# A two-layer graph network on one core: layer 0 started on half of the adjacency, the second group's neighbour lists made beside the first group's attention

## The chip, the core and the metric

The kernel runs on one core of a Trainium2 chip. A core has five engines that run beside each other, each working through its own queue of instructions in order: TensorE (PE in the profile; its weight loads are PEld), VectorE (DVE), ScalarE (ACT), GpSimd (POOL) and SyncE (SP, which here only issues DMAs). Data moves between HBM and on-chip memory by 16 DMA engines; a DMA can be issued from SP, ACT or POOL. The metric is device time in microseconds (us), and smaller is better.

## The reference

There are 3327 nodes with 512 features each and a symmetric 0/1 adjacency with self loops, about nine neighbours a node. Two layers follow each other, each with a residual and a layer norm.

```python
# layer 0: graph attention, 4 heads of 128
feats = einsum('nf,hfo->hno', x, W)
logits = leaky_relu(e_self[:, :, None] + e_neigh[:, None, :], 0.2), masked by adj
out0 = relu(concat_h(softmax(logits) @ feats) + b)
x = layernorm(x + out0)
# layer 1: a gated pair
attn_a = sigmoid(concat(adj @ x, x) @ Wa.T + ba);  attn_b likewise with Wb, bb
x_a = normalised(exp(-leaky_relu(s_left[:, None] + s_right[None, :], 0.01)) * adj) @ (x @ W_sa)
x_b = adj @ (x @ W_gcnb) + b_gcnb
x = layernorm(x + sigmoid(attn_a * x_a + attn_b * x_b))
```

All arithmetic that reaches the output is in float32.

## The kernel before, in words

The nodes, padded to 3328, are 26 tiles of 128. The kernel does not multiply with the adjacency: it turns it into lists of neighbours and gathers rows.

**First stage.** SP loads x (chunks of 512 nodes, three buffers, `load_x`) and the adjacency (`load_adj`, L197, chunks of 512 columns, each in 13 pairs of 128-row blocks, twelve buffers, so a pair is loaded when an earlier one has been used). TensorE does two kinds of work: `features(t)` (L307) projects tile t on the four heads and on the score columns, ScalarE copies the result out of PSUM, and POOL writes it as a row of 520 numbers to `table0` in HBM (L321); `make_codes(i)` (L333) sums the adjacency of chunk i into codes that hold 8 rows' bits and a block number, and `turn_codes` (L355) transposes them so that a node is a partition. VectorE then finds each node's neighbours: `top_codes` (L365, three rounds of the eight greatest, over 224 codes), `decode` (L371) and `pick` (L389, three rounds again, over 96 candidates), up to 24 neighbours a node. All 26 tiles go through this before attention.

**Groups and lists.** Nodes fall into two groups, the first 12 tiles (group 0) and the other 14 (group 1). In a group the nodes are sorted by number of neighbours: `rank_a` and `rank_b` (L416, L426) work out ranks on VectorE with two matmuls, `sort` (L455) scatters each list to its rank in HBM (one POOL scatter a tile, L137), and a DMA loads the sorted lists into `srt`. Sorted tile j needs only `CAPS[j]` neighbours a node: 22 for the first tile of each group, 4 or 5 for the last. For group 0 the x rows of the sorted nodes are gathered as well (`own_x`, L463, 12 POOL gathers); for group 1 SP copies x and the table rows side by side into `own1` (L512, L513), so that one gather brings both.

**Layer 0.** `gather(table0, j)` (L525) issues one indirect DMA on POOL for each neighbour slot (L546; L540 for the slot that comes from `own1`): 128 rows of 520 numbers. A buffer holds up to 6 slots, and there are 7 buffers. In iteration i of the loop at L689 the kernel emits, in this order: the gather of the tile three ahead; for finished groups of up to four tiles the `publish` (L656: ScalarE normalises, POOL scatters the row to `table1`); `columns2` of tile i-2; `attend` of tile i (L619: each row is multiplied with its weight on VectorE, every third one on ScalarE at L629, and TensorE adds it up in PSUM with an identity matmul, L634); for tile i-1 the residual (L704), the statistics and `columns1` (transposes); `columns3`; and the weighing of tile i+1 (`weigh_a`, `weigh_b`, L599: leaky ReLU and softmax of the scores). The order of the tiles is 11, 10, 0 to 9, 12 to 25. Each engine keeps this order, so an instruction that waits holds all behind it on its engine.

Group 1's list scatters are issued at L668, after the gathers of the first three tiles. Behind them the buffers of the first stage are given back, and VectorE clears `over` (L676) in their place.

**Layer 1.** The same gathers from `table1`, in another order of tiles; weights and gates on VectorE, sums on VectorE and TensorE, two projections by W_sa and W_gcnb (L831), and a scatter of the rows to the output. `covered` (L468) checks on the chip that no list was cut; if one was, a dense version of everything runs instead.

Of the kernel before, what the change touches and what calls it, by code (L numbers as in the profile page):

```python
# [34 lines left out]
CH = 512  # L35

# [40 lines left out]
def sparse_pass(  # L77
# [3 lines left out]
    x: bass.AP,  # L81
# [32 lines left out]

    nc = tc.nc
    N, F = out.shape
    NP = x.shape[0]
# [12 lines left out]
    table0 = dram.tile([NP, ROW], F32, name="table0")  # L130
    table1 = dram.tile([NP, ROW], F32, name="table1")
# [26 lines left out]
    selves = const.tile([P, NT], F32, name="selves")  # L158

# [4 lines left out]
    def own(j):  # L164
        g, i = place(j)
        return srt[g][:, i, 0:1]
# [30 lines left out]
    def load_adj(i):  # L197
        cw = min(CH, NP - chunks[i])
        for q, (a, b) in enumerate(pairs_of(NT)):
            at = p0.tile([P, 2, CH], F32, tag="at", name=f"at{i}_{a}", bufs=AT)  # L200
            nc.sync.dma_start(at[:, :, :cw], adjB[i, q] if cw == CH else adjL[q])

            ones_of = at.bitcast(BF16).rearrange("p t (n w) -> p t n w", w=2)[:, :, :cw, 1]
            loaded[i, a], loaded[i, b] = ones_of[:, 0], ones_of[:, 1]

    load_x(0)
    wsa0 = pj.tile([P, KT, F], F32, name="wsa0")
    nc.scalar.dma_start(wsa0, W_sa.rearrange("(k p) o -> p k o", p=P))
    asa_rows = []
    for s in range(2):  # L210
        a_row = pj.tile([P, F], F32, name=f"asa_row{s}")
        nc.scalar.dma_start(a_row, row_bcast(a_sa, F, s * F))
        asa_rows.append(a_row)
    load_x(1)
    for i in range(len(chunks)):
        load_adj(i)
        load_x(i + 2)
# [40 lines left out]
    nc.gpsimd.iota(st[:, :, 0], pattern=[[P, NT]], base=0, channel_multiplier=1)  # L258
    for g, n in enumerate(NG):
# [16 lines left out]
    nc.gpsimd.dma_start(table1[N:NP, :], zrow)  # L276
# [3 lines left out]

    nc.gpsimd.memset(v1, 0.0)
# [14 lines left out]
    for s in range(2):  # L296
        for k in range(KT):
            prod = pj.tile([P, F], F32, tag="prod1", name=f"sprod{s}_{k}", bufs=2)
            nc.gpsimd.tensor_mul(prod, wsa0[:, k], asa_rows[s])
            nc.vector.tensor_reduce(v1[:, k, 3 - 3 * s : 4 - 3 * s], prod, AX.X, ALU.add)  # L300

    nc.gpsimd.tensor_add(v1[:, :, 4:6], v1[:, :, 4:6], v1[:, :, 1:3])
    nc.gpsimd.tensor_add(v1[:, :, 6], v1[:, :, 0], v1[:, :, 3])

    deg = [p0.tile([P, n], F32, name=f"deg{i}") for i, n in enumerate(NG)]

    def features(t):  # L307

        i = t * P // CH
        xc = xcs[i]  # L310
        o = t * P - chunks[i]
        pf = psf.tile([P, 2, 512], F32, tag="pf", name=f"pf{t}")
        for k, hh in ((k, hh) for hh in range(2) for k in range(KT)):
            nc.tensor.matmul(  # L314
                pf[:, hh, :HC], xc[:, k, o : o + P], w0[:, k, hh, :], start=(k == 0), stop=(k == KT - 1)
            )
# [4 lines left out]
        nc.gpsimd.dma_start(table0[t * P : (t + 1) * P, :], row)  # L321
        if t == NT - 1:
            nc.gpsimd.dma_start(table0[N:NP, F : F + H], nrow[:, F : F + H])
# [4 lines left out]
    def span(i):  # L328

        t0 = chunks[i] // P  # L330
        return (t0, min(CH, NP - chunks[i]) // P, *place(t0))

    def make_codes(i):  # L333
# [3 lines left out]
        for half, ms in enumerate(halves):  # L337
            pc = psl.tile([P, CH], F32, tag=f"pc{half}", name=f"pc{half}_{i}")
            for m in ms:
# [5 lines left out]
                if s == 0 and own0 // 4 == m // 4:  # L345
                    for j in range(nt):
                        nc.tensor.matmul(
                            pc[32 * c : 32 * c + 32, j * P : (j + 1) * P], pow2[:, j, :], less1, start=False, stop=False
                        )
            w = widths[half]  # L350
            nc.scalar.activation(
                v[:w, half, : nt * P], pc[:w, : nt * P], AF.Identity, bias=blk[:w, half : half + 1]
            )
# [11 lines left out]
    def top_codes(i):  # L365

        ent = ents[i] = p0.tile([P, 4, S], F32, tag="ent", name=f"ent{i}", bufs=2)
        for j in range(span(i)[1]):
# [20 lines left out]
    def pick(i):  # L389
# [22 lines left out]
        nc.vector.tensor_scalar(st[:, t0 : t0 + nt, 1 : S + 1], some[:, :nt], float(N), None, ALU.add)  # L412
# [42 lines left out]
    def sort(g, ranki, queue):  # L455
# [4 lines left out]
        if g == 0:  # L460
            tasks.extend(lambda j=j: own_x(j) for j in range(NG[0]))

    def own_x(j):  # L463
        nc.gpsimd.indirect_dma_start(
            out=row1(j)[:, 0:F], out_offset=None, in_=x, in_offset=bass.IndirectOffsetOnAxis(ap=own(j), axis=0)
        )

    def covered():  # L468

        for g, n in enumerate(NG):  # L470
            nc.vector.tensor_scalar(valid[:, T0[g] : T0[g] + n, :], srt[g][:, :, 1 : S + 1], N, None, ALU.is_lt)
# [3 lines left out]
        nc.vector.tensor_mul(over, over, valid)  # L475
# [4 lines left out]
        pb = psx.tile([P, NCOL], F32, tag="pcol", name="pbad", bufs=2)  # L480
# [4 lines left out]
    ts = iter(range(NT))  # L485

    def more(n):
        for _ in range(n):
            t = next(ts, None)
            if t is not None:  # L490
                features(t)
                later(3)

    NC0 = NG[0] * P // CH
    assert NG[0] * P % CH == 0
    more(3)
    rankis = [None, None]
    for i in range(len(chunks)):
        make_codes(i)
        more(1)  # L500
        if i == NC0:
            rankis[0] = rank_b(0)
            sort(0, rankis[0], nc.gpsimd)
# [4 lines left out]
        if i == NC0 - 1:  # L508
            rank_a(0)
# [827 lines left out]
```

## Time and profile before

| what | value |
|---|---|
| median of 3 runs (lowest, highest) | 1033.98 us (1031.57 to 1038.35) |
| profiled execution, own time | 1029.15 us |
| its span, first to last instruction | 1027.4 us |
| busy share of the span | PE 79%, DVE 71%, POOL 64%, ACT 27% |
| mean granted TensorE clock | 0.899 |
| adjacency loads (L201) | 78 of 512 KB and 13 of 256 KB, issued from SP |
| gathers L546 | 496 on POOL, 1025 ns each, 508.2 us |
| first gather L546; first attention matmul L634 | 177.0 us; 246.7 us |
| last attention matmuls of layer 0 | from 589.0 us |

A line of the groups names the source line, the engine, the operation, what it writes and reads with shapes, how often, then the busy time and mean duration of one, and the idle time of that engine just before with what ended it. In a timeline each line is a start time, a length, the engine, the line and operation, and in brackets the idle time before it and its releaser; "issue" means that nothing the profile shows was waited for. A wait line gives who waited for whom, the total, how often, and the longest. The span starts at 0.

### The profile page before, as it was taken

The page shows a single profiled execution, that of the slowest core. Times are in us where ns is not written, and L with a number is a line of the kernel's source. Part 1 is how long each engine was busy: PE and PEld are TensorE (multiplying, and loading weights), DVE is VectorE, ACT ScalarE, POOL GpSimd, SP SyncE. Part 2 cuts the span into 40 slices and gives each one's busy share as a digit, 9 for nine tenths or more (in the row PEclk, how much of TensorE's full clock was granted, in tenths as well). Part 3 has the DMA queues.
Part 4 walks back from the last instruction along what each step waited for, and adds up shares of the span by engine and source line. Part 5 has one row for each costly group of instructions (what it writes and reads, how often), then busy time and mean ns, then how long its engine had stood idle before and what let it go on. Part 6 is the DMA issues. An engine that isn't in the chain of part 4 may idle for free.

```text
span 1027.4 us, 10026 instructions
## 1 busy us (share of the span) xinstructions
PE 810.6 (79%) x2564; PEld 420.8 (41%) x2564; DVE 732.5 (71%) x2128; ACT 273.9 (27%) x751; POOL 658.2 (64%) x673
## 2 busy tenths in 40 slices
PE   4698974203999983999699939996996989999994
PEld 3477751101444441444344414443442444444342
DVE  4387898704866760957466848886986989989894
ACT  1112210002344340353334413331131132232223
POOL 6411246773777777777777657777677677777602
PEclk9799995555999997899989969998998999999998
DMA  8999999993777678777777547778578566667501
GB/s 318 395 361 398 365 369 386 368 256 97 206 210 208 205 213 193 241 228 227 216 233 226 182 127 196 195 194 202 159 196 205 157 189 187 191 195 192 178 0 64
DMA packets 74193, 229.31 MB, mean 223 GB/s; under 512 B 13872, under 2 KB 18144, under 8 KB 73232
## 3 DMA queue, kind: packets, MB, share of 16 engines
q0 software_dynamic: 50240, 164.52, 55.8%
q1 hardware_dynamic: 22784, 61.97, 15.9%
q10 hardware_dynamic: 1104, 2.10, 0.6%
q8 instruction: 23, 0.38, 0.1%
q14 instruction: 42, 0.34, 0.1%
HBM read 207.46 MB, written 28.54 MB: 230 GB/s over the span
## 4 chain that ended last, share of the span: by engine, by line
PE 32%; POOL 12%; DMA 10%; issue 10%; DVE 9%; ACT 3%; DVEq 0%; POOLq 0%; ACTq 0%
PE acc L634 17%; POOL g L546 10%; DMA g<-table,srt 10%; PE acc L812 5%; PE po L831 4%; DVE sw L795 3%; PE pcol L650 2%; PE acc L623 2%; POOL out L137 1%; DVE g L797 1%; ACT xt L647 1%; PE pt L822 1%; PE x1t L643 1%; ACT za L872 1%; POOL g L540 1%
## 5 line engine op out<-in xcount | busy, mean ns | idle before, releaser
L546 POOL DMA_INDIRECT g<-table,srt x496 | 508.2, 1025 | 174.7 <-issue 128.3
L634 PE MATMUL acc<-g,ident 128*128 128x512 f32 x536 | 242.4, 608 | 41.1 <-DVE g L631 41.1
L795 DVE SCALAR_TENSOR_TENSOR sw<-g,e,sw 128x512 f32<-128x512 f32 x242 | 181.4, 749 | 16.4 <-ACT sw L784 11.8
L634 PEld LDWEIGHTS acc<-g,ident 128*128 128x128 f32 x536 | 105.0, 196 | 176.6 <-issue 107.4
L812 PE MATMUL acc<-g,ident 128*128 128x512 f32 x294 | 140.6, 610 | 20.3 <-DVE g L797 20.1
L631 DVE TENSOR_TENSOR g<-g,w 128x512 f32<-128x512 f32 x188 | 118.4, 698 | 0.7
L314 PE MATMUL pf<-w,xc 128*128 128x260 f32 x416 | 99.1, 399 | 13.5 <-DVE w L272 13.5
L629 ACT ACTIVATE g<-g,w 128x128 f32<-128x128 f32 x320 | 96.3, 389 | 1.9 <-DVE w L617 1.9
L812 PEld LDWEIGHTS acc<-g,ident 128*128 128x128 f32 x294 | 55.8, 194 | 99.0 <-issue 54.2
L831 PE MATMUL po<-wg,sT 128*128 128x512 f32 x208 | 94.7, 598 | 0.0
L831 PE MATMUL po<-wsa,sT 128*128 128x512 f32 x208 | 93.9, 594 | 0.2 <-ACT sT L824 0.2
L314 PEld LDWEIGHTS pf<-w,xc 128*128 128x128 f32 x416 | 81.4, 198 | 28.7 <-DVE w L272 14.3
L797 DVE TENSOR_TENSOR g<-g 128x512 f32<-128x512 f32 x95 | 65.7, 692 | 3.3
L650 PE MATMUL pcol<-v,xt 128*128 128x8 f32 x208 | 29.6, 269 | 46.6 <-ACT xt L647 46.6
L321 POOL DMA_DIRECT2D table<-row x26 | 14.4, 555 | 79.2 <-ACT st L320 79.2
L605 DVE TENSOR_TENSOR w<-g,srt 128x20 f32<-128x20 f32 (+3 forms) x57 | 9.9, 181 | 76.6 <-DMA g<-table,srt 71.3
L858 ACT ACTIVATE za<-za 128x512 f32<-128x512 f32 x26 | 16.4, 633 | 167.9 <-DVE za L856 167.9
L831 PEld LDWEIGHTS po<-wg,sT 128*128 128x128 f32 x208 | 40.1, 193 | 50.9 <-issue 50.6
L831 PEld LDWEIGHTS po<-wsa,sT 128*128 128x128 f32 x208 | 39.7, 191 | 50.4 <-issue 48.2
L137 POOL DMA_INDIRECT out<-za,srt x26 | 28.5, 1095 | 49.7 <-ACT za L872 43.0
L341 PE MATMUL pc<-at,pow 128*32 128x512 bf16 (+1 forms) x182 | 26.2, 421 | 31.9 <-DMA at<-in_adjB 25.3
L610 ACT ACTIVATE w<-w 128x40 f32<-128x40 f32 (+10 forms) x26 | 6.2, 237 | 166.5 <-DVE w L609 166.3
(186 smaller groups left out, 916.7 us busy)
## 6 DMA issues: line engine op xcount, KB each, us to landing
at<-in_adjB SPq DMA_DIRECT2D x78, 512.0 KB, 11.9
g<-table,srt POOLq DMA_INDIRECT x496, 3.8
table<-row POOLq DMA_DIRECT2D x26, 260.0 KB, 6.5
xc<-in_xB SPq DMA_DIRECT2D x6, 1024.0 KB, 9.6
own<-in_xo SPq DMA_DIRECT2D x1, 3640.0 KB, 32.4
own<-table SPq DMA_DIRECT2D x1, 3640.0 KB, 55.4
at<-in_adjL SPq DMA_DIRECT2D x13, 256.0 KB, 8.9
w<-in_W0B SPq DMA_DIRECT2D x1, 1040.0 KB, 6.9
```

Of the source, the lines that this page charges most:

```text
L137: put = nc.gpsimd.indirect_dma_start(out=dst, out_offset=bass.IndirectOffsetOnAxis(ap=rows, axis=0), in_=src, in_offset=None, bounds_check ...
L314: nc.tensor.matmul(pf[:, hh, :HC], xc[:, k, o : o + P], w0[:, k, hh, :], start=(k == 0), stop=(k == KT - 1))
L341: nc.tensor.matmul(pc[32 * c : 32 * c + 32, : nt * P], pow2[:, s, :], loaded[i, m], start=(s == 0), stop=(m + 1 not in ms or s == 3),)
L546: nc.gpsimd.indirect_dma_start(out=buf[:, q - q0, :], out_offset=None, in_=table[:, :], in_offset=bass.IndirectOffsetOnAxis(ap=srt[g][:, i ...
L629: nc.scalar.activation(gv[:, h, :], gv[:, h, :], AF.Copy, scale=w[:, s, h : h + 1])
L631: nc.vector.tensor_tensor(gv, gv, w[:, s, :].rearrange("p (h o) -> p h o", o=1).to_broadcast([P, H, FO]), ALU.mult)
L634: nc.tensor.matmul(acc, ident, buf[:, o + s - s0, 0:F], start=False, stop=(s == CAPS[j]))
L650: nc.tensor.matmul(pcol, xt1[:, k, :], v1[:, k, :], start=(k == 0), stop=(k == KT - 1))
L795: nc.vector.scalar_tensor_tensor(sw, g[:, i, 0:F], e[:, s : s + 1], sw, ALU.mult, ALU.add)
L797: nc.vector.tensor_add(g[:, i, 0:F], g[:, i - 1, 0:F], g[:, i, 0:F])
L812: nc.tensor.matmul(plain[j], ident, row, start=(not sums_of_two and i == 0), stop=(sums_of_two and i == len(rows) - 1),)
L831: nc.tensor.matmul(proj[j], sT[:, k, :], wt[:, k, :], start=(half + k == 0), stop=(half + k == KT))
```

## The change

1. The adjacency is cut into chunks of 4, 4, 2, 2, 4, 4, 4, 2 tiles of columns (`CT`); the first four are group 0. Only these are turned into codes and lists in the first stage. A generator yields after each pair of blocks, and a table `PACE` says how many pairs TensorE takes ahead of each feature tile. SP's loads are put in a fixed order that mixes x and adjacency; `wsa0` and `asa_row` move from ACT's queue to SP's, behind all x chunks. The layer-1 columns (`sprod`) are made by 4 products on POOL instead of 8 and at tile 20 instead of the start; their sums follow the ranking of group 0.
2. Chunks 4 to 7 (group 1) are turned into codes and lists inside the layer-0 loop, in iterations 1 to 6, and ranked and sorted in iteration 7 (`beside`). They stand behind `columns3` and ahead of the weighing of the next tile.
3. For group 0 the table holds x and features of a node in adjacent rows (`by_node`), x copied there by one DMA, and group 0's gather takes both with one indirect DMA, as group 1's does from `own1`. `own_x` is gone. Group 1's rows are written twice by POOL, to the table and to `own1`, and the copy at L513 is gone. The rows of x that layer 1 doesn't fill are set to ones by two DMAs.
4. In group 0 every second row is multiplied on ScalarE, instead of every third.
5. `over` is cleared by POOL at the start. The PSUM pool of the layer-0 columns has one buffer until group 1 is sorted, then two.

```diff
+CT = (4, 4, 2, 2, 4, 4, 4, 2)
+PACE = (0, 0, 0, 1, 3, 6, 8, 10, 13, 14, 17, 20, 23, 26, 29, 32, 36, 41, 45, 49, 52)
...
-    table0 = dram.tile([NP, ROW], F32, name="table0")
+    table0 = dram.tile([NP + R0, ROW], F32, name="table0")
+    by_node = [table[: 2 * R0].rearrange("(n t) w -> n t w", t=2) for table in (table0, table1)]
...
     load_x(0)
+    load_x(1)
+    load_adj(0)
+    load_x(2)
+    load_adj(1)
+    load_x(3)
+    load_x(4)
+    load_adj(2)
+    load_adj(3)
...
+    load_x(5)
+    load_x(6)
+    nc.sync.dma_start(wsa0, W_sa.rearrange("(k p) o -> p k o", p=P))
     for s in range(2):
+        nc.sync.dma_start(asa_rows[s], row_bcast(a_sa, F, s * F))
-    load_x(1)
-    for i in range(len(chunks)):
-        load_adj(i)
-        load_x(i + 2)
...
+    def columns_a():
+        for s, k in ((s, k) for s in range(2) for k in range(0, KT, 2)):
+            prod = sprods[s, k] = pj.tile([P, 2, F], F32, tag="prod", name=f"sprod{s}_{k}", bufs=4)
+            nc.gpsimd.tensor_mul(
+                prod, wsa0[:, k : k + 2], asa_rows[s].rearrange("p (k o) -> p k o", k=1).to_broadcast([P, 2, F])
+            )
...
-        nc.gpsimd.dma_start(table0[t * P : (t + 1) * P, :], row)
+        if t < NG[0]:
+            nc.gpsimd.dma_start(by_node[0][t * P : (t + 1) * P, 1, :], row)
+        else:
+            nc.gpsimd.dma_start(table0[R0 + t * P : R0 + (t + 1) * P, :], row)
+            nc.gpsimd.dma_start(own1[t * P - R0 : (t + 1) * P - R0, 1, :], row)
...
-        if g == 0:
-            tasks.extend(lambda j=j: own_x(j) for j in range(NG[0]))
...
+    nc.sync.dma_start(by_node[0][:, 0, :], xo[:R0])
+    for i in range(G0, len(CT)):
+        load_adj(i)
...
+    nc.sync.dma_start(own1[:, 0, :], xo[R0:])
...
+    for t in range(NT):
+        while pairs < PACE[min(t, len(PACE) - 1)]:
+            next(steps)
+            pairs += 1
...
+        if t < 2:
+            project0(t, F // 2, HC)
+        else:
+            project0(t, 0, HC)
+        features(t)
+        later(3)
+        if turning is not None:
+            lists_of(turning)
+            if turning == G0 - 1:
+                columns_a()
+                rank_a(0)
+            turning = None
+        if t == NT - 2:
+            rankis[0] = rank_b(0)
+            sort(0, rankis[0], nc.gpsimd)
+            columns_b()
...
-        ahead = 0 if table is table1 else 1 + g
+        ahead = 0 if table is table1 else 2
+        pairs, word = (by_node[0], 0) if g == 0 else (own1, S + 1)
...
-                if s % 3 == 2:
+                if s % (2 + (j >= NG[0])) == 1:
...
+    def codes_and(i, j1):
+        make_codes(i)
+        turn_codes(i)
+        top_codes(i, 0, j1)
+
+    def ends_of(i, j0):
+        top_codes(i, j0)
+        decode(i)
+        pick(i)
+
+    def sort1():
+        rank_a(1)
+        rankis[1] = rank_b(1)
+        sort(1, rankis[1], nc.sync)
+        later(len(tasks))
...
+    beside = {
+        1: lambda: codes_and(4, 2), 2: lambda: ends_of(4, 2), 3: lambda: codes_and(5, 2), 4: lambda: ends_of(5, 2),
+        5: lambda: codes_and(6, 2), 6: lambda: (ends_of(6, 2), codes_and(7, 2), ends_of(7, 2)), 7: sort1,
+    }
...
-            xj = y if j < NG[0] else got[j][0][2][:, 0, 0:F]
-            nc.vector.scalar_tensor_tensor(y, accs[j], 0.0, xj, ALU.max, ALU.add)
+            nc.vector.scalar_tensor_tensor(y, accs[j], 0.0, got[j][0][2][:, 0, 0:F], ALU.max, ALU.add)
...
         if 2 <= i < NT + 2:
             columns3(order0[i - 2])
+        if i in beside:
+            beside[i]()
         if i + 1 < NT:
             weigh_a(order0[i + 1])
             weigh_b(order0[i + 1])
```

## The prediction

> **What bounds the kernel now.** I read the page first, then the busy time by stretches, then GpSimd's (POOL's) timeline, then VectorE's (DVE's) timeline inside one adjacency chunk. The stretches are: 177 us (first neighbour gather) to the first attention matmul, layer 0 on group 0, layer 0 on group 1.
>
> ```profile
> 177.00:244.00 67.00, 7.52 (x18) 3.83 (x18) 23.47 (x122) 0.40 (x1) 48.83 (x50) 0.50 0.83 261
> 246.70:416.50 169.80, 141.81 (x407) 69.62 (x408) 103.08 (x278) 62.22 (x194) 123.09 (x126) 0.92 0.74 207
> 416.50:600.00 183.50, 163.27 (x493) 81.55 (x491) 126.95 (x394) 70.53 (x204) 131.07 (x132) 0.96 0.69 210
> ```
>
> Columns: stretch, length, busy PE, PE weight load, DVE, ACT, POOL, PE clock, DMA share, GB/s. From 177 to 244 TensorE and VectorE do almost nothing while POOL issues. VectorE is 61% busy in group 0, so nothing there runs it full.
>
> ```profile
> 176.98 0.96 POOL L546 DMA_INDIRECT g<-table,srt  x1 [0.30 <-issue]
> 178.25 0.95 POOL L546 DMA_INDIRECT g<-table,srt  x1 [0.30 <-issue]
> ...
> 255.33 0.99 POOL L546 DMA_INDIRECT g<-table,srt  x1 [14.58 <-PE acc L634]
> ...
> 375.18 0.95 POOL L540 DMA_INDIRECT g<-own,srt  x1 [0.30 <-DMA g<-table,srt]
> ```
>
> One gather costs POOL 1.26 us (start to start). Between 177 and 375 POOL stood still once, 14.58 us, for a buffer. So tile 12, the first of group 1, begins to be gathered at 375.2, and POOL goes on at the same step to about 580. Up to there POOL sets the pace; it had 36 gathers ahead when attention began, because VectorE was held:
>
> ```profile
> DVE over L676 <- issue: 39.6, 1, 39.6
> DVE ent L69 <- PE pv L361: 20.0, 4, 11.0
> ```
>
> The first line is the clearing of `over`, which waits for POOL's 14 list scatters; the second is the list search waiting for TensorE's transposes, also when a chunk had TensorE to itself. What the lists cost VectorE:
>
> ```profile
> 69.62 0.40 DVE L69 MAX8 ent<-pv 128x8 f32<-128x224 f32 x1 [2.64 <-PE pv L361]
> ...
> 78.31 0.29 DVE L376 CAST bn<-ent 128x96 int32<-128x96 f32 x1
> ...
> 81.99 0.25 DVE L392 TENSOR_REDUCE ovf<-code 128x4 f32<-128x96 f32 x1
> ...
> 89.87 0.21 DVE L412 TENSOR_SCALAR st<-some 128x96 int32<-128x96 f32 x1
> ```
>
> A chunk of four tiles takes 20.5 us without a gap: search 8.7 (2.17 a tile), decode 3.7, pick 8.1. In the first stage this hides under the load of the adjacency.
>
> **What the Trainium skill says.** Perfetto Trace Analysis, Sequencer Loop: instructions wait in their engine's queue for their semaphores. The trace agrees: one waiting clear at L676 held VectorE 39.6 us. DMA: Bandwidth & Descriptors, Anatomy of one DMA: a DMA's semaphore wait is done on the issuing sequencer; here POOL's 14.58 us. The same page, Issuing engines are not separate DMA queues: all engines' transfers interleave on the same 16. The trace agrees: beside loads and copies (177 to 222) a gather landed after 8.1 us (median), alone (270 to 370) after 3.7, at the same issue step. TensorE: Matmul & The Clock Gate, What's actually happening: an idle window of about 3.4 us halves the clock. Here, after 41 us idle, 6 rows took 8.34 us, the next 7 rows 6.17.
>
> **The change part by part.**
>
> *First stage.* 14 of 26 adjacency columns leave it. TensorE keeps 26 feature tiles (four took 14.22, so 3.56 each: 92), codes for 12 tiles (about 8), their transposes (3); starting at 9 instead of 12.9 (the first two tiles no longer wait for the score columns), 112. DMA keeps 1.0 MB of W0, 6.7 of x, 20 of adjacency, about 8.5 of row writes and vectors: 36 MB at 375 GB/s (mean of 25 to 175 us) is 97, plus 5, so the last x chunks land near 102 and their six tiles end at 122 at worst. I take 118. Then, in POOL's queue: copies out 0.9, row writes 1.1, the wait of the padding row for the last row 6.0 + 0.6, 12 scatters at 1.27 (15.3), 2.7 for their landing, list load 1.1 + 6.3: 34. The columns for layer 1 (4 products of 1024 at 2.45) now sit in that queue behind a late weight load: 0 to 10, I take 5. First gather 157 (148 to 163) instead of 177: 20 us earlier. The 12 gathers of x rows (12 x 1.26) and the SP copy of table rows go; they stood before 177, in that figure. The clears on POOL at the start (27, of 0.2) are covered by its 79.2 us of waiting for row copies.
>
> *Self rows.* One gather now brings x and features, so the count per tile stays (CAPS+1), but a group-0 tile takes CAPS+2 slots: tiles 10 and 11 together 4 buffers instead of 3. Its first buffer is also held until L704 reads x, after the next tile's multiplications.
>
> *Attention split.* In group 0 half of the rows instead of a third go to ScalarE: 4.78 us for 4 rows, 1.2 each, hidden under TensorE's 0.86 a row. VectorE: 0.64 a row.
>
> *Lists of group 1 beside attention.* In VectorE's order they stand between L704 of tile i-1 and the weighing of tile i+1, so all attention behind them waits. Durations are from VectorE's and TensorE's timelines between 284 and 305 us: L704 0.69, statistics 0.87, column copy 0.17; weighing 9 short instructions, 2.0 to 2.2 with ScalarE's exponential; norm 2.6; TensorE 0.86 a row (46 half matmuls in 19.74); ranking from the rows of L420 to L445, 0.5 and 4.2 plus gaps. Tile 0's gather (the 36th) is issued at 157 + 36 x 1.26 = 202, lands 7 later, and is weighed at 211. From there VectorE works, per iteration (rows x 0.64 + 1.8 for L704, statistics and column copy + 2.2 weighing + lists + norm or publish):
> i=2: 7.7+4.0+16.1 = 27.8. i=3: 4.5+4.0+4.3 = 12.8. i=4: 3.8+4.0+16.1+2.6 = 26.5. i=5: 3.8+4.0+4.3 = 12.1. i=6: 3.2+4.0+1.8+16.1+12.6 = 37.7. i=7, to the end of ranking: 3.2+1.8+0.5+4.5 = 10.0. Sum 127. In four of them it also waits for TensorE, because codes and transposes stand in TensorE's queue behind the whole attention of tile i. At i=3: 13 rows (11.2) + first row and its transposes 2.5 + codes, copy and turn 4 = 18, less VectorE's 6.5 until then: 11. At i=5 likewise 10, at i=6 0, at i=7 7 (10 rows 8.6 + 3 - 5). 28. Two adjacency chunks come through what the gathers leave (390 - 207 = 183 GB/s; 13 pairs are 37 us) and add some 2.5 each: 5. TensorE is idle for 8 to 25 us before tiles 1, 3, 5 and starts at half clock, 2 each: 6. Ranking ends at 211 + 127 + 28 + 5 + 6 = 377.
>
> *POOL behind it.* 14 scatters wait for the ranking: 17.8, then tile 9's 7 gathers 8.8, so tile 12 starts at 404 instead of 375: 29 later. SP loads the new lists while those 7 gathers run. Tile 12 then meets fewer free buffers, since held ones come free only with the next tile: 5 for tile 13. After that the order is that of before. The end check does a pass less on VectorE (0.6), nothing else in layer 1 changes.
>
> Sum: -20 at the first gather, +49 by tile 12, +5 buffers: +34. Profiled execution 1029.15 (span 1027.4) becomes 1063. The median of the runs, 1033.98, is 4.8 above that execution: 1068.
>
> **Rivals.**
>
> *The same, with DMA as a second bound* (0.19). For: 0.74 of DMA is taken by gathers alone, and some 24 MB of adjacency and fills come on top. Gathers land at 9 instead of 7 and only 140 GB/s are left: +12 to +25, so 1080 to 1093. Against: from 177 to 222 the loads beside gathers left the issue step at 1.26.
>
> *The lists overlap* (0.17): VectorE never waits for TensorE. Then ranking is at 211 + 127 = 338, tile 12 at 365, -10 and 5 for buffers: 1029. With the first gather at 148 instead of 157 it is 1020, faster. It decides from the point where at most a fifth of the 39 us of waits is left. Against: L69 already waited for the transposes.
>
> *POOL stays the bound* (0.06), the other side: nothing holds POOL from the first gather on. 148 + 125 x 1.26 + 8 publishes x 1.3 + 14 scatters 17.8 = 334 for tile 12 instead of 375: 993. It needs the ranking by 316, that is 105 us of VectorE after tile 0, where the list has 127.
>
> *The change doesn't shorten the first stage* (0.03): TensorE's and POOL's order give nothing, first gather at 177: 1088.
>
> **How the numbers follow.** The likeliest (0.55) is 1068, own range 1050 to 1085. About 1% is what a measurement here tells from no change: 1023.6 to 1044.3. Faster: POOL bound 0.06 and a quarter of the overlap, 0.10. Same: the rest of the overlap and a little of the likeliest, 0.14. Slower 0.76. Range 1036 to 1096, leaving out POOL bound, most of the overlap and small tails.
>
> **What would show it.** First gather at 148 to 163, first attention matmul near 175; VectorE over 85% busy from tile 0 to the ranking, with waits of 6 to 12 us of L69 for `pv`; TensorE idle before tiles 3, 5, 6 and 7; POOL waiting over 20 us ahead of the list scatters; L540's group-1 gathers from about 404; layer 1 as long as before. It is wrong if POOL's step stays unbroken, or if the first stage ends more than 15 us from 157.

## The result, and the profile after

The changed kernel takes 1082.6 us (median of 4 runs, 1077.72 to 1083.34), the kernel before beside it 1034.24: ratio 1.045 (95% interval 1.041 to 1.050), 48 us slower. Its profiled execution took 1081.86 us with a span of 1080.1, against 1029.15 and 1027.4 before. The kernels below ran on several chips. On those of a2, e4, e5, e6, f2, f3 and g1 the kernel before took 1033.5 or 1033.6 us; they are called the faster chips. e1, e2, e3 and f1 ran on a slower chip (kernel before: 1137.56 us) and f5 on another slower one (1134.12 us). Ratios are to the kernel before on the same chip, and the kernel before has no trace on the slower chips. The ratios leave out runs that took over 1.5% longer than the fastest of their kernel, which came up on the slower chips only, while the medians hold all runs.

First POOL's timeline in the changed kernel, at the four places that the prediction priced.

```profile
162.25 1.01 POOL L612 DMA_INDIRECT g<-table,srt  x1 [3.60 <-DMA srt<-lists]
...
389.63 1.00 POOL L146 DMA_INDIRECT lists<-st,ranki  x1 [0.37 <-DVE w L677]
...
407.38 0.97 POOL L146 DMA_INDIRECT lists<-st,ranki  x1 [0.30 <-issue]
...
417.71 0.95 POOL L612 DMA_INDIRECT g<-own,srt  x1 [0.30 <-issue]
...
465.70 0.95 POOL L618 DMA_INDIRECT g<-table,srt  x1 [7.27 <-DVE x1a L789]
```

The first gather starts at 162.25 (predicted 157; before 176.98), group 1's list scatters at 389.63 (predicted 377), tile 12 at 417.71 (predicted 404; before 375.18). Later, at 465.70, POOL stands 7.27 us for a first buffer that the residual L789 still holds. The last attention matmuls of layer 0, in the changed kernel and in the kernel before:

```profile
641.55 4.46 PE L706 MATMUL acc<-g,ident 128*128 128x512 f32 x10
```

```profile
589.00 4.45 PE L634 MATMUL acc<-g,ident 128*128 128x512 f32 x10
```

They end at 646.0 instead of 593.5. From there to the end both kernels take the same: 434.1 and 433.9 us. So the whole loss, 52.7 us by the spans, arises before layer 1, and since the first gather is 15 us earlier, layer 0 from its first gather on takes 67 us longer.

Then the busy time by stretches of the changed kernel (columns as in the prediction): first gather, tile 0 weighed, half of the list work, ranking done, tile 12, end of layer 0.

```profile
162.00:223.00 61.00, 20.14 (x72) 9.51 (x72) 15.08 (x50) 9.80 (x30) 42.65 (x45) 0.61 0.89 246
223.00:305.00 82.00, 58.86 (x176) 28.82 (x175) 60.34 (x226) 30.03 (x99) 45.24 (x48) 0.83 0.94 344
305.00:389.00 84.00, 50.70 (x178) 26.11 (x178) 53.78 (x200) 24.99 (x74) 28.74 (x30) 0.74 0.61 195
389.00:418.00 29.00, 25.14 (x75) 13.31 (x76) 22.37 (x73) 16.51 (x50) 22.24 (x23) 0.88 0.38 110
418.00:646.00 228.00, 183.88 (x529) 91.21 (x528) 127.43 (x391) 86.85 (x264) 162.01 (x163) 0.90 0.72 215
```

From 223 to 389 POOL, which stood still once on this way in the kernel before, works 74 us of 166 and VectorE 114. Neither is full: the queues wait for each other. The waits from 162 to 440 say which:

```profile
DVE ent L72 <- PE pv L408: 45.3, 4, 16.3
...
POOL g L612 <- DVE x1a L789: 33.4, 4, 13.5
...
POOL g L618 <- DVE x1a L789: 16.3, 2, 8.3
PE pc L380 <- DMA at<-in_adjB: 12.0, 3, 5.1
...
DVE tots L489 <- PE tot L485: 9.4, 1, 9.4
```

Each of the four chunks has one long wait of the list search (L72) for TensorE's transposes (L408), except the last with 0.43. While VectorE stands there, the residual and the weighing behind it in its queue stand too, so buffers stay full and POOL waits for L789.

### The profile page after: what moved, and what is told of

It is laid out like the page before. It is cut to its first block, busy times and chain, and to the rows that moved or that the text cites. A ratio compares the mean times of both kernels' runs of the same rounds, so it can differ in the third digit from the quotient of the medians.

```text
span 1080.1 us, 10313 instructions
## 1 busy us (share of the span) xinstructions
PE 828.4 (77%) x2622; PEld 434.0 (40%) x2622; DVE 720.5 (67%) x2106; ACT 306.3 (28%) x865; POOL 654.2 (61%) x698
## 4 chain that ended last, share of the span: by engine, by line
PE 33%; POOL 20%; issue 17%; DMA 14%; DVE 12%; ACT 3%; POOLq 0%; DVEq 0%; ACTq 0%; SPq 0%
POOL g L618 15%; DMA g<-table,srt 12%; PE acc L706 11%; PE pf L343 6%; PE acc L899 5%; PE po L918 5%; POOL lists L146 2%; PE pcol L722 2%; PE acc L695 2%; DVE sw L882 2%; DVE ent L72 1%; DVE topv L75 1%; ACT xt L719 1%; POOL out L146 1%; DMA xc<-in_xB 1%
## 5 line engine op out<-in xcount | busy, mean ns | idle before, releaser
L618 POOL DMA_INDIRECT g<-table,srt x484 | 497.1, 1027 | 200.9 <-issue 139.8
L706 PE MATMUL acc<-g,ident 128*128 128x512 f32 x536 | 251.5, 627 | 37.6 <-DMA g<-table,srt 37.6
L706 PEld LDWEIGHTS acc<-g,ident 128*128 128x128 f32 x536 | 109.5, 205 | 182.3 <-issue 150.4
L899 PE MATMUL acc<-g,ident 128*128 128x512 f32 x294 | 141.9, 615 | 20.3 <-DVE g L884 20.2
L701 ACT ACTIVATE g<-g,w 128x128 f32<-128x128 f32 x432 | 129.0, 389 | 3.8 <-DVE w L689 2.6
L722 PE MATMUL pcol<-v,xt 128*128 128x8 f32 x208 | 35.4, 298 | 115.2 <-ACT xt L719 115.2
L343 PE MATMUL pf<-w,xc 128*128 128x260 f32 (+2 forms) x448 | 103.5, 386 | 10.8 <-DMA xc<-in_xB 10.8
L677 DVE TENSOR_TENSOR w<-g,srt 128x20 f32<-128x20 f32 (+3 forms) x59 | 10.5, 181 | 134.9 <-DMA g<-table,srt 133.9
L703 DVE TENSOR_TENSOR g<-g,w 128x512 f32<-128x512 f32 x160 | 99.7, 691 | 0.7
L899 PEld LDWEIGHTS acc<-g,ident 128*128 128x128 f32 x294 | 56.3, 196 | 99.8 <-issue 55.2
L343 PEld LDWEIGHTS pf<-w,xc 128*128 128x128 f32 x448 | 83.6, 196 | 28.1 <-issue 15.8
L722 PEld LDWEIGHTS pcol<-v,xt 128*128 128x128 f32 x208 | 33.0, 242 | 122.0 <-ACT xt L719 122.0
L72 DVE MAX8 ent<-pv 128x8 f32<-128x224 f32 x26 | 10.1, 387 | 82.7 <-PE pv L408 82.7
```

The source lines that it names most:

```text
L343: nc.tensor.matmul(pfs[t][:, hh, n0:n1], xcs[i][:, k, o : o + P], w0[:, k, hh, n0:n1], start=(k == 0), stop=(k == KT - 1),)
L618: nc.gpsimd.indirect_dma_start(out=buf[:, q - q0, :], out_offset=None, in_=table[:, :], in_offset=bass.IndirectOffsetOnAxis(ap=srt[g][:, i ...
L701: nc.scalar.activation(gv[:, h, :], gv[:, h, :], AF.Copy, scale=w[:, s, h : h + 1])
L703: nc.vector.tensor_tensor(gv, gv, w[:, s, :].rearrange("p (h o) -> p h o", o=1).to_broadcast([P, H, FO]), ALU.mult)
L706: nc.tensor.matmul(acc, ident, buf[:, o + s - s0, 0:F], start=False, stop=(s == CAPS[j]))
L722: nc.tensor.matmul(pcol, xt1[:, k, :], v1[:, k, :], start=(k == 0), stop=(k == KT - 1))
```

## The experiments

**Theory A (the queue theory):** the list work stands in VectorE's and TensorE's order, where it delays the attention behind it and waits behind the attention ahead of it; that holds the ranking, and with it POOL. **Theory B (the DMA theory):** the adjacency loads beside the gathers make both late.

**e1.** The four products for layer 1's columns go to VectorE, after group 0's ranking.

```diff
-    def columns_a(): (four nc.gpsimd.tensor_mul at tile 20)
     def columns_b():
-        for (s, k), prod in sprods.items():
+        for s, k in ...:
+            nc.vector.tensor_mul(prod, wsa0[:, k : k + 2], asa_rows[s]...)
```

> The changed kernel with the four layer-1 products (L322) made by VectorE after group 0's ranking, instead of by POOL at tile 20. If they cost what the trace of the changed kernel shows (three list instructions L425 to L428 at 5.5 us instead of 0.6 beside POOL's products, and feature rows queued behind them), group 0's ranking comes 5 us earlier, the first gather falls from 162 to about 157, and the time from 1082 to about 1077. If what delays the first gather is the load of x or the features themselves, the first gather stays at 160 or later and the time within 2 us.

Measured on the slower chip: first gather at 155.14, 2 us better than expected; 1169.32 us, ratio to before 1.037 (1.023 to 1.051). The changed kernel did not run on that chip, so what the edit is worth to the whole is answered by g1 below.

**e2 and e3.** e2 leaves out the search of chunks 5 to 7 (copies of chunk 4's lists stand in for it), e3 the loads of these chunks (chunk 4's blocks stand in); in both the rest is as in the changed kernel.

```diff
-    3: lambda: codes_and(5, 2), 4: lambda: ends_of(5, 2), ...
+    3: lambda: codes_only(5), 4: lambda: copied(5), ...    # e2, and so for 6 and 7
-    for i in range(G0, len(CT)): load_adj(i)
+    load_adj(G0)                                           # e3, the others reuse its blocks
```

> The changed kernel with the list search of chunks 5 to 7 left out on VectorE: their lists are copies of chunk 4's, so the output differs for group 1, and the result of the check for cut lists is set to zero. Loads, codes and transposes stay. Queue theory (list work in VectorE's order holds up the attention behind it): 85 us of work and waits leave VectorE's chain in iterations 3 to 6, POOL becomes the bound, tile 12's first gather comes at 345 to 360 instead of 418, time 1012 to 1025. DMA theory (adjacency loads beside the gathers cost the time): at most 10 us less than 1082.

> The changed kernel with the adjacency loads of chunks 5 to 7 left out: their codes are made from chunk 4's blocks (one pair standing in for the first one), so the lists of group 1 differ and the result of the check for cut lists is set to zero. All list work stays. Queue theory: only the waits for pairs (4.8, 2.1, 3.6) and the late landing of tile 0 (about 7) go, tile 12's first gather at 400 to 406, time 1064 to 1070. DMA theory: most of the 42 us by which tile 12 is late goes, time 1040 to 1050.

Measured, on the slower chip, one run each: e2 1146.25 us with tile 12 at 407.06; e3 1168.32 with tile 12 at 436.31. e1, with all loads and all list work, had tile 12 at 430.96. Taking the loads away left tile 12 no earlier, taking the search away made it some 24 us earlier. Their first gathers differ (155.14 in e1, 162.23 in e2, 167.33 in e3); counted from there, tile 12 comes after 275.8 us in e1, 244.8 in e2 and 269.0 in e3, so by this count, from one run each, the loads are worth some 7 us and the search some 31. But the changed kernel itself was not run on that chip, so the size stayed open, and the times that both expectations name, which were for a faster chip, can't be held against it.

**f1.** The kernel before with one part of the change: POOL clears `over` at the start.

```diff
+    nc.gpsimd.memset(over, 0.0)
+    ... nc.gpsimd.memset(over[:, j, c:S], 1.0)
-    nc.vector.memset(over, 0.0)      # at L676, behind 14 list scatters
```

> The kernel before with one part of the change alone: `over` is cleared by POOL at the start and not by VectorE behind group 1's list scatters. Attention should start near 200 instead of 246.7. If POOL sets the pace of layer 0, only its one stop of 14.6 us goes and the time falls from 1034 to about 1019. If VectorE's late start costs more than that, about 1005; if POOL meets new waits for buffers, 1025 to 1034.

Measured, on the slower chip: 1125.45 us, ratio 0.992 (0.988 to 0.995), so 1% faster than the kernel before there. This part of the change gains on that chip; on a faster one it was not tried alone. The first attention matmul is at 248.4 and not near 200, because VectorE was still at the lists. Its timeline in f1 has gaps between the instructions of its own search:

```profile
209.18 0.40 DVE L69 MAX8 ent<-topv 128x8 f32<-128x224 f32 x1 [2.34 <-remote]
...
213.39 0.39 DVE L69 MAX8 ent<-topv 128x8 f32<-128x224 f32 x1 [2.35 <-remote]
```

From 183 to 232 it is busy for 10.6 us of 49, in list work alone. The kernel before and f3, on faster chips, have no such gaps in this work. What the gaps wait for is not shown. In f3, which holds the same edit, the matmuls of this ranking start at 201.9, in f1 at 238.9.

**a2.** The changed kernel again, beside e5, e6 and f2 on one of the faster chips.

> The changed kernel itself, beside the kernels below on the same chip. Both theories: 1075 to 1090 us where the kernel before takes 1034 (ratio 1.04 to 1.05); first gather at 162, tile 12's first gather at 418.

Measured: 1084.25 us, ratio 1.050 (1.046 to 1.054); first gather 161.67, list scatters from 391.85, tile 12 at 419.92. It is the reference for the next runs.

**e5.** Code sums and transposes ahead of the attention matmuls in TensorE's queue; VectorE's order is untouched.

```diff
+    early = {1: lambda: codes(4), 3: lambda: codes(5), 5: lambda: codes(6), 6: lambda: codes(7)}
...
+        if i in early:
+            early[i]()
         if 2 <= i < NT + 2:
             columns2(order0[i - 2])
```

> The code sums and the transposes of chunks 4 to 7 stand on TensorE's queue ahead of the attention matmuls of iterations 1, 3, 5 and 6 instead of behind them; the search stays where it is on VectorE. Theory A (the list search waits behind TensorE's attention matmuls, which in turn wait for gathers and multiplications): the waits of the first search of a chunk for its transposes, 45 us over four chunks in the changed kernel, nearly go; ranking ends some 20 to 26 us earlier, tile 12's first gather at 392 to 398 instead of 418, the whole 1055 to 1063 where the changed kernel takes 1082. Theory B (adjacency loads and gathers share the DMA engines, and the late transfers set the pace): the code sums then wait for their adjacency blocks in front of the attention matmuls; ranking ends no earlier, 1078 to 1095.

Measured: 1062.76 us, ratio 1.028 (1.024 to 1.032), 21.5 us less than a2. The waits of e5 from 162 to 440:

```profile
PE pc L380 <- DMA at<-in_adjB: 12.8, 3, 4.9
DVE tots L489 <- PE tot L485: 8.7, 1, 8.7
...
DVE ent L72 <- PE pv L408: 4.9, 1, 4.9
```

The search's waits fall from 47.3 us (a2) to 4.9; the scatters start at 369.90 (22 us earlier) and tile 12 at 398.21. TensorE's waits for adjacency blocks of both sizes are no longer than in the changed kernel (15.1 us against 15.6), though it now meets them earlier. Theory A holds, and its size at the slow end of what was expected for tile 12 and for the whole.

**e6.** Left out: code sums, transposes and search of chunks 4 to 7. The loads, the ranking and the scatters stay.

```diff
-    beside = {1: lambda: codes_and(4, 2), 2: lambda: ends_of(4, 2), ... 7: sort1}
+    beside = {1: copied1, 7: sort1}
```

> Left out: code sums, transposes and search of chunks 4 to 7 (group 1 gets copies of group 0's lists, so its outputs differ); the adjacency loads stay, and the 14 list scatters, the ranking and all gathers stay. Theory A (the list work in VectorE's and TensorE's order delays the ranking): the ranking ends when VectorE gets to it after iteration 7's attention, POOL paces with 1.26 us a gather, tile 12's first gather comes 162 + 198 + 18 = 378 or a little earlier, 40 us before the changed kernel's 418, and the whole takes 1035 to 1045 where the changed kernel takes 1082. Theory B (the loads beside the gathers are what costs): tile 12 still after 400, and 1065 or more.

Measured: 1031.46 us, ratio 0.999 (0.997 to 1.001). POOL in e6:

```profile
169.09 1.01 POOL L612 DMA_INDIRECT g<-table,srt  x1 [6.97 <-DMA at<-in_adjB]
...
356.81 0.96 POOL L146 DMA_INDIRECT lists<-st,ranki  x1 [0.30 <-issue]
...
366.93 0.95 POOL L612 DMA_INDIRECT g<-own,srt  x1 [0.30 <-issue]
```

The loads are all there, and no code sum holds them back for buffers, so they come even denser (the first gather itself is 7 us later for it); from the first gather to tile 12 POOL takes 198 us, as in the kernel before. Theory B falls: the loads alone don't make tile 12 late. The time is 4 us below theory A's range too, with tile 12 at 367 where 378 was expected. And it shows how little there was to win: with group 1's code sums and search for nothing, the changed kernel is level with the one before.

**f2.** All eight chunks' lists ahead of the first gather, as before; the x copy for group 0 stands in SP's queue ahead of chunks 6 and 7. Of the change it keeps the new chunks, the x rows in the table, ScalarE's larger share and the early clear of `over`. The order of the loads, the place of the layer-1 products and SP's copy of table rows into `own1` are again much as before.

```diff
-    steps = all_steps() ... (codes of chunks 0 to 3 in the feature loop)
+    for i in range(len(CT)):
+        make_codes(i); more(1); ...; lists_of(i); more(CT[i])
...
-    beside = {1: ..., 7: sort1}
+    sort(1, rankis[1], nc.sync)      # behind the first three tiles' gathers
```

> All eight chunks' lists before the first gather, as in the kernel before, with the rest of the change kept: x rows in the table, the flags of free slots cleared at the start by POOL. x copy of group 0 sent by SP ahead of the adjacency of chunks 6 and 7. Theory A (the change loses by placing the list work beside attention, the rest of it gains): first gather some 9 to 10 us earlier than in the kernel before (8 of its 12 gathers of x rows came after the last row write), the clearing of the flags 12 us (as measured alone, ratio 0.992), 1008 to 1018 where the kernel before takes 1034. Theory C (the x copy ahead of the last adjacency blocks, or the first buffers held for the residual, cost as much): 1022 to 1035.

Measured: 1056.21 us, ratio 1.021 (1.017 to 1.025); both theories missed. POOL in f2:

```profile
171.59 1.03 POOL L595 DMA_INDIRECT g<-table,srt  x1 [0.65 <-DMA at<-in_adjB]
...
244.90 0.95 POOL L601 DMA_INDIRECT g<-table,srt  x1 [32.82 <-PE acc L689]
...
252.46 1.00 POOL L146 DMA_INDIRECT lists<-st,ranki  x1 [0.30 <-issue]
...
391.37 0.95 POOL L595 DMA_INDIRECT g<-own,srt  x1 [0.31 <-PE pcol L705]
```

The first gather is 5 us earlier, not 9 to 10. SP issues the last chunk's loads from 174.4 on instead of 150.8 (behind a 3 MB copy and in eight chunks instead of seven), so the lists are late, the first attention matmul comes at 236.6 (only 10 us earlier than before, with no clear of `over` to wait for), and POOL, whose first three tiles now need eight buffers of the seven, stands 32.82 us with the scatters queued behind that gather. So x rows in the table are not free either: they need an extra buffer early, and 3 MB in a first stage in which DMA is 97% busy. How f2's loss splits between these was not measured.

**e4.** ScalarE copies a tile's x rows out of the first buffer when its attention begins, so the residual no longer holds that buffer.

```diff
+        nc.scalar.copy(row1(j)[:, 0:F], got[j][0][2][:, 0, 0:F])
         acc = accs[j] = ps.tile(...)
-            nc.vector.scalar_tensor_tensor(y, accs[j], 0.0, got[j][0][2][:, 0, 0:F], ALU.max, ALU.add)
+            nc.vector.scalar_tensor_tensor(y, accs[j], 0.0, y, ALU.max, ALU.add)
```

> The changed kernel, but ScalarE copies a tile's x rows out of its first gather buffer when its attention begins, and the residual reads that copy: the first buffer no longer stays held until the residual. Theory A (the held buffers delay the gathers): POOL's waits for the residual, 33 and 16 us between 162 and 440 in the changed kernel, turn into shorter ones for the last attention matmul of a tile; tile 12's first gather unmoved or a few us earlier, since the ranking sets it, and group 1 gains the 10 us that it lost after tile 12: 1068 to 1076 where the changed kernel takes 1083. Theory B (the waits for buffers are slack beside VectorE's and TensorE's order): 1080 to 1088, some of it for 26 more copies on ScalarE.

Measured: 1077.44 us, ratio 1.044 (1.040 to 1.048), 7 us less than a2 (the profiled executions differ by 10). The scatters start at 392.66, now after a wait of 4.34 us for VectorE, and tile 12 at 420.28, not earlier; but from tile 12 to the end of layer 0 it is 218.7 us, where a2 takes 228.5 and the kernel before 218.3. POOL's waits of e4 from 162 to 440:

```profile
POOL g L618 <- issue: 81.2, 108, 19.7
...
POOL g L612 <- PE acc L707: 11.5, 1, 11.5
...
POOL g L618 <- PE acc L707: 6.0, 5, 4.7
```

The waits for L789 are gone, others stand in their place ("issue" of up to 19.7 us), because there the pace comes from VectorE's list work. Only where that is past does the freed buffer count, and there it gives back the 10 us that the change loses behind tile 12. The time is 1.4 us slower than theory A's range.

**g1.** e5 and e1 together.

> The early code sums and transposes (1063 us, ratio 1.028), and beside them the four products for layer 1's columns on VectorE after group 0's ranking instead of on POOL at tile 20. Theory A (those products hold the last row writes and stretch the list instructions of the last chunk of group 0): first gather at 155 instead of 162, and all of it reaches the end: 1054 to 1058. Theory B (what comes after is set by the adjacency blocks and not by the first gather): first gather at 155, but 1060 to 1065.

Measured: 1054.72 us, ratio 1.021 (1.018 to 1.024); first gather at 155.12, tile 12 at 390.11. The 7.4 us at the first gather reach the end in full (8.0). The best of the versions with lists beside attention is still 21 us behind the kernel before.

**f3.** f1, with the 12 gathers of x rows behind the first three tiles' gathers.

```diff
-            tasks.extend(lambda j=j: own_x(j) for j in range(NG[0]))
...
+    for j in order0[: NG[0]]:
+        own_x(j)
     sort(1, rankis[1], nc.sync)
```

> The kernel before with its flags of free slots cleared at the start by POOL (ratio 0.992), and with the 12 gathers of group 0's x rows moved behind the neighbour gathers of the first three tiles. Theory A (POOL's gathers set layer 0's pace, so it is their number that counts): first gather 9 us earlier (168), tile 12's first gather hardly earlier than with the flags alone (some 360), 1017 to 1025 where the kernel before takes 1034. Theory B (the start of attention counts): 1008 to 1016.

Measured, on a faster chip: 1031.14 us, ratio 0.998 (0.997 to 1.000), above both ranges. POOL in f3:

```profile
166.47 1.04 POOL L549 DMA_INDIRECT g<-table,srt  x1 [5.11 <-DMA at<-in_adjL]
...
227.34 0.95 POOL L467 DMA_INDIRECT x1a<-in_x,srt  x1 [2.35 <-DMA g<-table,srt]
...
372.71 0.95 POOL L543 DMA_INDIRECT g<-own,srt  x1 [0.30 <-issue]
```

The first gather is 10.5 us earlier and the first attention matmul 35 (211.4 instead of 246.7), tile 12 only 2.5. POOL takes 206 us between them: 198.2 as before, less the stall of 14.58, plus 12 gathers (15.1), plus 7.4 of waiting for earlier gathers to land. That is theory A's mechanism: POOL's own work sets the pace, and an early start of attention alone brings nothing. What the expectation left out is that in the kernel before, five of these 12 gathers (from 153.8 to 160.5) stood ahead of the last row write, where POOL had nothing else to do.

**f5.** f1, with the table's row for absent neighbours written at the start.

```diff
+    nc.gpsimd.dma_start(table0[N:NP, :], nrow)                  # at the start
-        nc.gpsimd.dma_start(table0[t * P : (t + 1) * P, :], row)
-        if t == NT - 1:
-            nc.gpsimd.dma_start(table0[N:NP, F : F + H], nrow[:, F : F + H])
+        rows = min(P, N - t * P)
+        nc.gpsimd.dma_start(table0[t * P : t * P + rows, :], row[:rows])
```

> The kernel before with its flags of free slots cleared at the start by POOL (ratio 0.992), and with the row of the table for absent neighbours written at the start, so that POOL does not stand for 6 us on the last rows' landing while gathers of x rows are queued behind it. Theory A (POOL's work between the last row write and tile 12 sets layer 0): first gather 171 to 173 instead of 177, tile 12's first gather at 355 to 358 instead of 375, 1013 to 1020 where the kernel before takes 1034. Theory B (the first gather waits for the landing of the last row anyway, and only the flags count): 1021 to 1026.

Measured, on the other slower chip: 1129.46 us, ratio 0.996 (0.993 to 1.000). First gather at 173.74 (f1, on its chip: 180.65), tile 12 at 402.77 (f1: 403.46). The first list scatter of f5 shows where the 7 us went:

```profile
247.98 1.00 POOL L137 DMA_INDIRECT lists<-st,ranki  x1 [29.26 <-DVE ranki L450]
```

In f1 this wait was 19.27 us. On both chips the ranking of group 1 comes at 245 to 248, so an earlier first gather is only a longer wait there. VectorE has the gaps of f1 in f5 too, and in both runs they begin 2 to 3 us after the first gather and end some 8 us after the last of the first three tiles' 36 gathers (f1: 183 to 232, f5: 176 to 226): with earlier gathers the gaps only came earlier. This says nothing of the faster chips, where the scatters of the kernel before start at 223.15 without a wait for the ranking; for those, neither theory is tested. f1 has the lowest ratio of all versions, on its chip.

## Why the prediction was right

**The sum.** Forecast +34 to the profiled execution, measured +52.7; the median 1068 against 1082.6. The likeliest case came true in its mechanism, and the time lies in its own range of 1050 to 1085, near the upper end. Of the 18.7 us that the sum lacks, some 5 are the first gather, 7 the weighing of tile 0, 1 POOL's part behind the ranking and 5 the buffers, all in the same direction; the chain from tile 0 to the ranking came out as forecast. By steps:

*First gather, −20.* It was −14.7, and two terms make up the difference. The last feature tile ends at 125.9 even without the products (g1), where I took 118, and POOL's part behind it takes 29 us instead of 34: two errors of 8 and 5 that largely cancel, which is luck. The rest is the four products: 7 us (first gather at 162.25, in g1 at 155.12) instead of 5. I gave them 0 to 10 us in POOL's queue and looked at no other engine, and it is not in that queue that they cost it. The changed kernel, POOL and VectorE, 108 to 118 us, and VectorE in g1, without the products:

```profile
108.81 9.28 POOL L322 TENSOR_TENSOR sprod<-wsa,asa_row 128x1024 f32<-128x1024 f32 x4 [1.85 <-DMA asa_row<-in_a_sa]
```

```profile
112.56 0.97 DVE L425 CAST bn<-ent 128x48 int32<-128x48 f32 x1
113.57 2.27 DVE L426 TENSOR_SCALAR bn<-bn 128x48 int32<-128x48 int32 x1
115.87 2.29 DVE L428 TENSOR_TENSOR code<-ent,bn 128x48 f32<-128x48 f32 x1
118.20 0.19 DVE L432 TENSOR_SCALAR bit<-code 128x48 int32<-128x48 int32 x1
```

```profile
112.55 0.19 DVE L422 CAST bn<-ent 128x48 int32<-128x48 f32 x1
112.78 0.19 DVE L423 TENSOR_SCALAR bn<-bn 128x48 int32<-128x48 int32 x1
113.00 0.21 DVE L425 TENSOR_TENSOR code<-ent,bn 128x48 f32<-128x48 f32 x1
```

A product takes 2.3 us (9.28 / 4), and while they run three list instructions take 0.97, 2.27 and 2.29 us. In g1 the same three take 0.19, 0.19 and 0.21. The Trainium skill says this (SBUF — State Buffer, Who interferes with whom): VectorE and GpSimd share a pair of SBUF ports as an exclusive lock, casts, tensor_scalar and two-input operations from SBUF can need it, and the loser waits for the whole instruction. The trace agrees: the last two each last one product long, while the MAX8 of L72 from 110.0 kept its 0.40. The prediction did not use it. The 5 us delay group 0's ranking, TensorE waits 6.85 us for it (L485; 1.94 in g1) with the last feature tile behind it, which then takes 4.98 us instead of 3.67, and POOL's last row write comes at 134.3; in g1 it is at 126.9. e1 and g1, with the first gather at 155, show the term.

*Tile 0 weighed at 211.* Its weighing starts at 220.76 and ends at 223. The last of its gathers, and the instruction of VectorE that waits for it:

```profile
206.34 0.95 POOL L618 DMA_INDIRECT g<-table,srt  x1 [0.30 <-issue]
```

```profile
220.76 0.18 DVE L677 TENSOR_TENSOR w<-g,srt 128x24 f32<-128x24 f32 x1 [11.95 <-DMA g<-table,srt]
```

Up to this gather, the 36th, POOL kept its step of 1.26 us, so 5 of the 12 us are the later first gather. The other 7 are its landing: it came some 13 us after the issue, where I took 7. Beside the loads the median of a landing was 7.1 us (162 to 302). From 209 to 223 POOL itself waited seven times, 6.8 us in all, for earlier gathers, which the reading of the kernel before (loads leave the issue step at 1.26 us) had not led me to expect; but these are gathers of tile 1, behind tile 0's.

*Tile 0 to ranking, 166 us* (127 of VectorE's work, 28 and 5 of waits, 6 of slow clock). Measured from 223.1 to 389.4 it is 166.3, of which 41.5 are waits for TensorE (16.34, 15.34, 0.43 and 9.39, forecast 11, 10, 0 and 7) and 125 the rest. The 41.5 stand for the forecast's 28 + 5 + 6 = 39; in them are 6.9 us in which TensorE itself waited for adjacency blocks (4.82 and 2.05), forecast 5. That the search would wait behind TensorE's attention was the step everything hung on; e5 shows it, 21.5 us of the whole. That "VectorE is over 85% busy" is wrong: it is 69% (114 of 166 from 223 to 389). By the prediction's own sum it could be no more than 77% (127 of 166), and the 127 also hold gaps between instructions and the exponential's round trip, which are no busy time. Likewise "almost nothing" was too strong for VectorE in the kernel before: its line from 177 to 244 has 23.5 us of 67.

*POOL waiting over 20 us ahead of the scatters.* It waited 0.37 us there. Its long waits came earlier, 49.7 us for buffers that the residual L789 held. Both come from VectorE's chain: in e4, where the residual holds no buffer, the scatters start no earlier.

*POOL behind it, +27.* Scatters and tile 9's gathers took 28.1 us (389.6 to 417.7).

*Buffers, +5.* It was 10 (228.3 against 218.3 from tile 12 to the end of layer 0), and e4 shows that the held first buffers are the cause of the 10: without them it is 218.7.

*Layer 1 unchanged:* 434.1 against 433.9.

**What the runs add to it.** At tile 12 the changed kernel (a2) stands at 420, e5 at 398, e6 at 367, the kernel before at 375. So of the 53 us between a2 and e6, 22 come from where TensorE's part stood in its queue. The other 31 go with the code sums and the search themselves; how much of them is pure work is not shown, since e5 still has 4.9 us of the search's waiting and 15.1 us of TensorE's waiting for blocks. (Counted from each one's own first gather, 161.67, 162.49 and 169.09, the two parts are 22 and 38.) In the first stage it had run beside loads that keep DMA 97% busy up to the first gather: taking 14 of 26 tiles of columns and the x gathers out of that stage advanced the first gather by only 15 us, or 22 with e1's edit.

**The rivals.** *DMA as a second bound* fell as the main mechanism (e6), though its time, 1080 to 1093, holds the result. The loads' share that the trace shows is the 7 us of late landing at tile 0 and the 6.9 us of TensorE's waits for blocks. *The lists overlap* would have needed e5's order, and even there 31 us over e6 stay. *POOL stays the bound*: e6 is that case, and it gives 1031, not 993, because its first gather is at 169 and not at 148, and POOL also waits for a buffer (7.4 us) and for landings (9.1).

**What stays open.** ScalarE's larger share (every second row in group 0) and the PSUM pool of one buffer were not tried alone; e6 holds both and takes 198 us from first gather to tile 12, as before. The time of f1 on a faster chip, how f2's loss splits, and what VectorE waited for in its gaps on the slower chips are open too.

## What to carry to other kernels

Work that runs beside a transfer can cost far more beside a chain of engines that already sets the pace. Here group 1's list work cost 53 us beside attention, and taking it out of the first stage, with its loads, gave 15 to 22. It costs still more if the queue puts it behind what it does not depend on. Before moving a block, ask on each engine what stands ahead of it in the queue and what stands behind: moving only the TensorE part to the front of its iteration (e5) was worth 21.5 us. A start that comes earlier is worth nothing if the queue that sets the pace still has the same work to do: f3 moved the first gather by 10.5 us and tile 12 by 2.5. And a trace from another chip can be held back by something else, as f1 and f5 were: compare it only with what ran there.

## What the runs showed of the hardware that was not expected

Three VectorE instructions of 0.2 us took 0.97 to 2.29 us beside POOL's products of 2.3 us each, while MAX8 beside them kept 0.40 us. Gathers of 128 rows that landed after 3.8 us (median over the kernel before) took 7.1 beside the adjacency loads of the changed kernel, and there single gathers waited 0.4 to 1.8 us at POOL for the landing of earlier ones. The same kernel before took 1034 us on some chips and 1134 to 1138 on two others. In f1 and f5, which ran on those two, VectorE stood up to 2.4 and 3.1 us between instructions of its own list work while the first three tiles' gathers ran, which in f1 filled most of the time from 183 to 232 us; in the kernel before and in f3, on faster chips, this work had no such gaps. Whether the chip is their cause is not shown.
